# Twenty idle transposes per step on TensorE in the first stage of a recommender scoring kernel

## The chip, the cores and the metric

The kernel runs on one core of one Trainium2 chip. The metric is the device time of one execution in microseconds (us), as the median of several runs.

## What is computed

There are 1024 sequences of 50 item numbers, and a table of 100001 items by 128 numbers whose row 0 counts as zero. The reference, cut to what matters:

```python
emb = emb_table.at[0].set(0.0)
e = emb[seq]                                   # 1024 x 50 x 128
prefix = jnp.cumsum(e, axis=1)
uF = prefix / jnp.minimum(t_idx, lengths)      # running mean per step
mean, var = uF.mean(axis=0), uF.var(axis=0)    # over the 1024 sequences
y = (uF - mean) * lax.rsqrt(var + BN_EPS) * gamma + beta
def step(v, x):                                # 50 steps, one after the other
    v = v + (x - v) / TAU
    spike = (v - V_TH >= 0)
    return v - spike * V_TH, spike
_, spikes = lax.scan(step, v0, moveaxis(y, 1, 0))
scores = spikes.mean(axis=0) @ emb.T           # 1024 x 100001
```

## The kernel before

The program has two stages. The **first stage** walks through the 50 steps and counts spikes; the **second stage** multiplies the counts by the table and writes 410 MB of scores. The order of instructions on every engine is the order of the Python code: it is written out by hand, and no planner moves anything.

In the first stage the layout is 128 features on the partitions and 1024 sequences along the free dimension, in two halves of 512. A step `t` works like this:

- **Gather.** POOL issues eight indirect DMAs (line 207), each of which fetches 128 table rows into a piece of the tile `e_t`. The pool `gather` has two buffers. `gather(t + 2)` stands behind step `t`'s transposes in the code and takes the buffer of `e_t`, so its first DMA waits until TensorE (PE) has finished with `e_t`.
- **Transposes.** PE transposes the eight pieces onto a running sum in PSUM, `pre[0]` and `pre[1]` (line 324, four pieces for each half). Each transpose waits for its own piece to land.
- **Running mean.** VectorE (DVE) turns each half of `pre` into `uF` (line 335) and takes its statistics (line 336). The first `uF` of a step waits for the fourth transpose, the second for the eighth.
- **Corrections.** `correct(t + 1, l)` (line 282) issues two matmuls of 128x512 onto `pre`, which take the table's row 0 out again where a sequence has item 0. Each of them overwrites what `uF` has just read, so it waits for that `uF`.
- **Rest of the step.** DVE and ScalarE (ACT) make the scale, the membrane value `v`, the count and the part that is left over (lines 342 to 379, 294, 298 and 301). They need neither PE nor POOL.

So on PE one step is: eight transposes of `e_t`, two corrections for step `t + 1`, eight transposes of `e_{t+1}`, and so on. In steps 42 and 44 the function `prepare` (lines 136, 152, 153) puts another eight transposes, of table rows into a PSUM tile `pt`, behind the corrections; ACT and DVE copy that tile.

PSUM has eight banks: two for `pre`, four for the two `v` tiles, and two for a tile `warm`. `warm` is written by a helper that is used in the last step only, and nobody reads it:

```python
def keep_busy(tile, times):
    for k in range(times):
        nc.tensor.transpose(warm[:, k % KQ * P : (k % KQ + 1) * P], tile, ident)
```

`KQ` is 8 and `P` is 128. In the second stage PE multiplies parts of the table by the counts, ACT and DVE take turns in copying PSUM to SBUF, and SP's queue writes the scores.

Of the kernel before, what the change touches and what calls it, by code (L numbers as in the profile page):

```python
# [24 lines left out]
KQ = HALF // P  # L25
# [14 lines left out]
def rec_kernel(  # L40
# [34 lines left out]
    ident = const.tile([P, P], F32, tag="ident", name="ident")  # L75
# [96 lines left out]
    with ExitStack() as ph:  # L172
# [107 lines left out]
        def correct(t, l):  # L280
            for h in range(B // BANK):
                nc.tensor.matmul(  # L282
                    pre[h],
                    lhsT=l,
                    rhs=zT[:, h * BANK : (h + 1) * BANK],
                    start=t == 0,
                    stop=False,
                    skip_group_check=True,
                )
# [18 lines left out]
# [3 lines that stand above are left out]
# [6 lines left out]
        for t in range(T):  # L317
# [20 lines left out]
                gather(t + 2)  # L338
            if not last:
                correct(t + 1, l)  # L340
            mv = sp.tile([P, 2], F32, tag="mv", name=f"mv_{t}")
            nc.vector.bn_aggr(mv, bs.rearrange("p h s -> p (h s)"))  # L342

# [210 lines left out]
```

## Time and profile before

| what | value |
|---|---|
| median of 3 runs | 1633.66 us (1633.3 to 1634.7) |
| the profiled execution: device time | 1638.64 us |
| the profiled execution: span from first to last instruction | 1636.8 us |
| last gather of the first stage issued at | 564.2 us |
| mean granted TensorE clock over the span | 0.799 |
| busy share PE / DVE / ACT / POOL | 66% / 58% / 41% / 23% |
| written to HBM | 409.6 MB |

A profile shows one execution. Busy shares are averages over both stages, so they say little about either of them. In the page's row of 40 slices each slice is 40.9 us long: the first 14 slices are the first stage, in which POOL is busy, and in the others POOL has nothing to do and the DMA engines move about 420 GB/s. The times of a PE instruction in the profile are those of its start, and of an end that is modelled and not observed.

### The profile page before, as it was taken

To read this page: it belongs to the slowest core of one execution; us is meant where nothing else is said; L and a number is where in the kernel's file an instruction comes from. 1 tells how busy PE (TensorE), PEld (TensorE's weight loads), DVE (VectorE), ACT (ScalarE), POOL (GpSimd) and SP (SyncE) were. 2 spreads that over 40 slices of the span, in tenths; PEclk is the share of its full clock that TensorE was granted. 3 is DMA by queue.
4 is the path that set the end of the run, shared out by engine and by line. 5 is a ranking of instruction groups with operands and counts; after the bars stand their busy time and mean duration, and the time that the engine had idled before them with its cause. 6 is when DMAs were issued, how large, how long until landed. Compare 5 with 4: busy or idle time off the path is not lost.

```text
span 1636.8 us, 12254 instructions
## 1 busy us (share of the span) xinstructions
PE 1085.8 (66%) x4464; PEld 806.9 (49%) x4464; DVE 948.7 (58%) x1127; ACT 673.0 (41%) x697; POOL 381.1 (23%) x406
## 2 busy tenths in 40 slices
PE   4333332333332488888988877888878888788884
PEld 2212111222112366666766666666666666566663
DVE  5666654677665865665755554555545555555652
ACT  2333322333323354555554444444444444444442
POOL 7666666766666500000000000000000000000000
PEclk7555555555555599999999999989999999999998
DMA  9611111111111279999999999999999999999998
GB/s 346 240 46 46 46 45 46 51 45 47 45 46 47 66 326 412 415 423 412 405 426 430 427 428 429 403 432 426 418 428 420 408 423 426 427 424 408 429 401 358
DMA packets 51313, 488.12 MB, mean 298 GB/s; under 512 B 10079, under 2 KB 10336, under 8 KB 30004
## 3 DMA queue, kind: packets, MB, share of 16 engines
q1 hardware_dynamic: 30752, 430.86, 62.6%
q0 software_dynamic: 12800, 26.24, 5.4%
q10 hardware_dynamic: 7700, 30.23, 4.5%
q8 instruction: 35, 0.57, 0.1%
q14 instruction: 26, 0.21, 0.0%
HBM read 77.69 MB, written 409.60 MB: 298 GB/s over the span
## 4 chain that ended last, share of the span: by engine, by line
DMA 42%; PE 16%; DVE 14%; another core or an unknown queue 9%; POOL 7%; issue 5%; ACT 5%; ACTq 0%; SPq 0%; DVEq 0%; POOLq 0%
DMA scores<-o 40%; PE po L160 14%; POOL e L207 7%; DVE o L512 3%; ACT o L514 3%; DVE uF L335 2%; DVE bs L336 2%; DMA e<-in_L_rec_emb_table,idx 2%; DVE v L379 2%; DVE negv L298 1%; ACT v L376 1%; PE pre L324 1%; DVE count L301 1%; DVE pairs L153 1%
## 5 line engine op out<-in xcount | busy, mean ns | idle before, releaser
L512 DVE TENSOR_SCALAR o<-po 128x1024 f32<-128x1024 f32 (+1 forms) x391 | 467.4, 1214 | 326.0 <-DMA scores<-o 183.8
L514 ACT ACTIVATE o<-po 128x1024 f32<-128x1024 f32 x391 | 391.8, 1025 | 503.9 <-DMA scores<-o 358.6
L207 POOL DMA_INDIRECT e<-in_L_rec_emb_table,idx x400 | 380.4, 951 | 183.5 <-issue 110.9
L160 PE MATMUL po<-pairs,countB 128*128 128x512 f32 (+1 forms) x1120 | 291.2, 406 | 61.1 <-ACT o L514 61.1
L160 PE MATMUL po<-pairs,countC 128*128 128x512 f32 (+1 forms) x840 | 237.8, 430 | 59.0 <-ACT o L514 53.1
L160 PEld LDWEIGHTS po<-pairs,countB 128*128 128x128 f32 x1120 | 210.4, 193 | 122.0 <-ACT o L514 80.0
L282 PE MATMUL pre<-zT,ls 128*128 128x512 f32 x100 | 78.4, 786 | 271.2 <-DVE uF L335 227.2
L160 PEld LDWEIGHTS po<-pairs,countC 128*128 128x128 f32 x840 | 166.2, 205 | 111.0 <-ACT o L514 65.0
L282 PEld LDWEIGHTS pre<-zT,ls 128*128 128x128 f32 x100 | 29.0, 291 | 309.9 <-DVE uF L335 255.7
L324 PE MATMUL pre<-ident,e 128*128 128x128 f32 x400 | 126.8, 435 | 79.5 <-DMA e<-in_L_rec_emb_table,idx 63.0
L335 DVE SCALAR_TENSOR_TENSOR uF<-rlen,pre 128x512 f32<-128x512 f32 x100 | 68.0, 680 | 161.7 <-remote 124.4
L324 PEld LDWEIGHTS pre<-ident,e 128*128 128x128 f32 x400 | 80.4, 209 | 126.8 <-DMA e<-in_L_rec_emb_table,idx 94.7
L153 DVE TENSOR_TENSOR pairs<-pt,pairs 128x1024 fp32r<-128x1024 f32 x70 | 85.3, 1218 | 96.1 <-ACT pairs L152 96.0
L346 ACT ACTIVATE r<-mv,eps 128x1 f32<-128x1 f32 x50 | 14.8, 295 | 273.0 <-DVE mv L342 181.0
L136 PE MATMUL pt<-ident,rows 128*128 128x128 f32 (+1 forms) x768 | 105.6, 283 | 9.9 <-issue 4.9
L136 PEld LDWEIGHTS pt<-ident,rows 128*128 128x128 f32 (+1 forms) x768 | 95.1, 148 | 27.4 <-issue 11.5
L160 PE MATMUL po<-hi,countB 128*128 128x512 f32 x208 | 85.4, 411 | 13.9 <-ACT o L514 13.6
L152 ACT CAST pairs<-pt 128x1024 fp32r<-128x1024 f32 x70 | 70.1, 1013 | 41.0 <-PE pt L136 41.0
L160 PE MATMUL po<-lo,countB 128*128 128x512 f32 x208 | 83.2, 400 | 0.0
L294 ACT ACTIVATE d<-v,less 128x1024 bf16<-128x1024 f32 x49 | 54.5, 1113 | 65.4 <-DVE v L379 36.3
L160 PE MATMUL po<-hi,countC 128*128 128x512 f32 x156 | 66.5, 426 | 14.2 <-ACT o L514 12.6
L376 ACT ACTIVATE v<-uF,hgb,a 128x1024 f32<-128x1024 f32 x49 | 59.2, 1208 | 31.0 <-DVE a L372 11.7
(88 smaller groups left out, 887.2 us busy)
## 6 DMA issues: line engine op xcount, KB each, us to landing
scores<-o SPq DMA_DIRECT2D x96, 3072.0 KB
scores<-o SPq DMA_DIRECT2D x32, 1536.0 KB
scores<-o SPq DMA_DIRECT2D x30, 1024.0 KB
rows<-in_L_rec_emb_table ACTq DMA_DIRECT2D x19, 1536.0 KB
scores<-o SPq DMA_DIRECT2D x8, 2896.5 KB
rows<-in_L_rec_emb_table SPq DMA_DIRECT2D x5, 3072.0 KB
e<-in_L_rec_emb_table,idx POOLq DMA_INDIRECT x400
rows<-in_L_rec_emb_table SPq DMA_DIRECT2D x2, 1024.0 KB
```

The source lines that it names most:

```text
L136: nc.tensor.transpose(pt[:, k0 : k0 + pw], r[:pw, k0 : k0 + D], ident[:pw, :pw])
L152: nc.scalar.copy(vh, vp)
L153: nc.vector.tensor_tensor(vl, vp, vh.bitcast(F32), ALU.subtract)
L160: nc.tensor.matmul(po[:, :kw], lhsT=counts[n], rhs=part[:, k0 : k0 + kw], start=j == 0, stop=j == 1,)
L207: nc.gpsimd.indirect_dma_start(out=es[t][:, n * P : (n + 1) * P], out_offset=None, in_=table, in_offset=bass.IndirectOffsetOnAxis(ap=idx[: ...
L282: nc.tensor.matmul(pre[h], lhsT=l, rhs=zT[:, h * BANK : (h + 1) * BANK], start=t == 0, stop=False, skip_group_check=True,)
L294: nc.scalar.activation(d, v, AF.Identity, bias=less)
L324: nc.tensor.matmul(pre[h][:, k : k + P], lhsT=e[:, h * BANK + k : h * BANK + k + P], rhs=ident, start=False, stop=last, is_transpose=True, ...
L335: nc.vector.scalar_tensor_tensor(uF[:, cs], rlen[:, cs], 1.0 / (t + 1), pre[h], ALU.max, ALU.mult)
L376: nc.scalar.activation(vt, uF[:, cs], AF.Identity, bias=hgb[:, 1:2], scale=a)
L512: nc.vector.tensor_scalar_mul(o[:, h0 : h0 + hw], po[:, :hw], 1.0 / T)
L514: nc.scalar.mul(o[:, h0 : h0 + hw], po[:, :hw], 1.0 / T)
```

## The change

One line is added behind the corrections of each step but the last:

```diff
             if not last:
                 correct(t + 1, l)
+                keep_busy(ident, 2 * KQ + KQ // 2)
             mv = sp.tile([P, 2], F32, tag="mv", name=f"mv_{t}")
             nc.vector.bn_aggr(mv, bs.rearrange("p h s -> p (h s)"))
```

In 49 steps PE gets twenty more transposes of the identity (line 310), each a weight load and a 128x128 matmul in float32, written to the two banks of `warm`. They wait for nothing, nobody waits for them, and nobody reads what they write. On PE they stand between the corrections for step `t + 1` and the transposes of `e_{t+1}`. The instructions of the other engines are the same, in the same order. Behind that line, all line numbers of the changed kernel are higher by one.

## The prediction

> **What bounds the kernel now.** I read the page's slices first. POOL works in the first 14 slices of 40.9 us; from there on the DMA row stands at 9 with about 420 GB/s. The second stage is bound by writing 409.6 MB and the change does not touch it, so a microsecond that the first stage ends later is a microsecond on the total. Then the groups.
>
> ```profile
> POOL 7666666766666500000000000000000000000000
> PEclk7555555555555599999999999989999999999998
> ...
> L207 POOL DMA_INDIRECT e<-in_L_rec_emb_table,idx x400 | 380.4, 951 | 183.5 <-issue 110.9
> ...
> L335 DVE SCALAR_TENSOR_TENSOR uF<-rlen,pre 128x512 f32<-128x512 f32 x100 | 68.0, 680 | 161.7 <-remote 124.4
> ```
>
> A gather takes 0.95 us and the next starts 0.30 us later (110.9 us of "issue" over 364 gaps): 1.25 us each, 10.0 us for the eight of a step. 400 of them fill 499 us, but the last one is issued at 564.2. So POOL's stream sets the end of the stage, and about 60 us of it are gaps. The waits tell which:
>
> ```profile
> POOL e L207 <- remote: 50.0, 10, 5.8
> POOL e L207 <- PE pre L282: 13.7, 3, 5.4
> ...
> DVE uF L335 <- remote: 124.4, 18, 10.0
> ```
>
> Thirteen times POOL stands for 2.5 to 5.8 us, 63.7 us in all. It waits for PE to be done with the buffer of two steps before. DVE's `uF` waits for PE too, up to 10 us. Yet PE is mostly idle. The timeline of steps 42 and 43, where `prepare` has eight more transposes, shows the riddle:
>
> ```profile
> 490.67 0.80 PE L282 MATMUL pre<-zT,ls 128*128 128x512 f32 x1 [1.14 <-DVE uF L335]
> ...
> 496.34 1.94 PE L136 MATMUL pt<-ident,rows 128*128 128x128 f32 x8 [4.87 <-issue]
> ...
> 498.07 1.80 PE L324 MATMUL pre<-ident,e 128*128 128x128 f32 x8
> ...
> 506.12 0.95 POOL L207 DMA_INDIRECT e<-in_L_rec_emb_table,idx  x1 [0.30 <-issue]
> 512.33 1.01 ACT L152 CAST hi<-pt 128x1024 fp32r<-128x1024 f32 x1 [15.11 <-remote]
> 512.84 0.94 POOL L207 DMA_INDIRECT e<-in_L_rec_emb_table,idx  x1 [5.76 <-remote]
> 513.37 1.22 DVE L153 TENSOR_TENSOR lo<-pt,hi 128x1024 fp32r<-128x1024 f32 x1 [17.14 <-ACT hi L152]
> 514.51 0.68 DVE L335 SCALAR_TENSOR_TENSOR uF<-rlen,pre 128x512 f32<-128x512 f32 x1
> ```
>
> By its records PE is through with all sixteen transposes at 499.9. Everyone who waits for them starts at 512.3 or later: the copy of `pt`, POOL, `uF`. PE reports its work done 12 us late, and does so 5.2 us after POOL has issued its last gather (507.07). In all of the long stalls POOL stops first and PE's reports come some 4 to 6 us later. In the trace's semaphore updates of such stretches PE reports one instruction per 2.1 to 2.8 us (325.9 and 328.7, say) while gathers run, then a handful within 0.2 us once they have stopped.
>
> When does this come? I counted PE's instructions between the stalls. From one restart of POOL to the next stop there are mostly four sets of gathers, 39.6 to 39.9 us, and 39 or 40 PE instructions (ten per step). The lag shows from about the 28th on. After the restart at 512.84 the second `prepare` comes early, and POOL stops after two sets, 19.7 us, with 28 instructions:
>
> ```profile
> 517.15 1.91 PE L324 MATMUL pre<-ident,e 128*128 128x128 f32 x8
> ...
> 528.75 1.94 PE L136 MATMUL pt<-ident,rows 128*128 128x128 f32 x8 [3.31 <-DVE count L301]
> 530.48 1.91 PE L324 MATMUL pre<-ident,e 128*128 128x128 f32 x8
> ...
> 533.76 0.69 DVE L335 SCALAR_TENSOR_TENSOR uF<-rlen,pre 128x512 f32<-128x512 f32 x1 [0.42 <-PE pre L324]
> ```
>
> Here PE ran sixteen transposes in one go, and the fourth of the `e` ones (start 531.12) was reported at 533.74. I read this as a **backlog**: reports leave at one per 2.45 us while gathers run, and some 20 may be outstanding (28 in 19 us less 19/2.45 = 8; 32 in 24 us less 10) before PE's progress becomes visible only at that rate. The stop of the gathers empties it. What holds the reports up the trace does not name; that the count is of instructions, whether they signal or not, rests on the two `prepare` steps, since of the eight transposes of `pt` only the last signals.
>
> **What the Trainium skill says.** "Perfetto Trace Analysis", Per-instruction lifecycle, Tensor Engine Instruction: the profile's end of a matmul is computed, and the semaphore goes out only once PSUM has acknowledged the write. The trace agrees: 499.9 against 512.3. "TensorE: Matmul & The Clock Gate", Part 1: the array runs at half clock until it has been busy for about 3.4 us. The PEclk row agrees (5 through the stage). Part 4 of that page says that transposes don't count for this; the windows disagree, as the sixteen transposes are followed by one window at full clock, though reports still stood still in it:
>
> ```profile
> 496.20:499.60 3.40, 3.26 (x16) 3.27 (x16) 0.04 (x1) 1.01 (x1) 2.77 (x3) 0.50 0.20 58
> 499.60:503.00 3.40, 0.27 (x2) 0.00 (x0) 0.00 (x0) 0.00 (x0) 2.50 (x3) 1.00 0.19 55
> ```
>
> **The change part by part.** Nothing is removed or moved; 49 x 20 = 980 transposes are added. Back to back, one starts each 0.213 us at half clock (eight in 1.91 us with the last one's 0.42), so twenty hold PE for 4.3 us, or about half of that where the clock rises. Behind them on PE stand the transposes of `e_{t+1}` (and `pt` in steps 42 and 44), and behind these the next corrections; DVE's `uF` and POOL's `gather(t + 3)` wait for those transposes.
>
> *As PE time it costs nothing.* Where nothing is late, `uF` starts every 7.35 us (301.70, 309.05), bound by DVE. With twenty more between, from `uF` of half 0: 2.0 us to the second correction, 0.6 for it, 4.3, three transposes (0.64), 0.5 to the report: 8.0 us. The gathers take 10.0, so POOL covers it. If that cover is gone, the price is 0.65 us a step.
>
> *As backlog it costs.* A step goes from 10 to 30 PE instructions. After an emptying, two corrections, twenty idle ones and the first transposes of `e_{t+1}` reach the limit within some 7 us (22 less 3). The eighth transpose is then not reported while the eight gathers in progress run, and POOL stops behind every set rather than behind every fourth. One set lasts 10.0 + 5.0 us. The 5.0 is the usual stall (4.5 to 5.8, mean 5.3 of the eleven long ones) less the 0.3 of an ordinary gap. Sets 2 to 49 wait for a buffer; I leave out the first two of these, where the backlog only builds up: 46 x 5.0 = 230 us. Of before, 63.7 - 13 x 0.3 = 60 us go. Sum: **+170 us**. On the profiled execution that is a span of 1807 and a device time of 1809; the median of the runs is 5.0 below the profiled one, so 1804. The last step and the second stage stay as they are. Bounds of the unknown stall: 2.5 us (the shortest) gives 46 x 2.2 - 60 = +41; 7.5 us, if more unreported work takes longer to clear, gives 46 x 7.2 - 60 = +271.
>
> **The rivals.**
> 1. *Idle transposes cure the stalls.* The late reports often begin when PE is nearly idle, one transpose per landing gather; a PE that is kept busy would report at once. Then POOL never stops: -60 us, 1574. It needs only that the density of PE's work decides, in the wait of line 207. Against it: sixteen in a row at 528.75 were late at once, and sixteen at 496.34, full clock included, freed nothing. The point from which it decides: fewer than 13 stalls are left.
> 2. *Only instructions that signal or wait count.* Then PE's idle time hides all: within 3 us, about 1634. For it speaks that idle ones carry no semaphores; against it, the `pt` transposes, seven of eight without.
> 3. *A larger limit for plain instructions.* POOL stops behind every second set: 24 x 5.0 - 60 = +60, 1694.
> 4. *Longer stalls*, as bounded above: 1905, or more.
>
> **How the numbers follow.** Backlog with a stall per set 0.58, every second set 0.11, longer stalls 0.10, the cure 0.17, hidden 0.04. The likeliest gives 1804. The range reaches from just under the +41 bound to the +271 one, 1665 to 1905, which takes in the first two and part of the third; the cure stays out. 0.2% (3.3 us) is what a measurement of this kernel can tell from no change. Faster 0.17, same 0.04, slower 0.79.
>
> **What would show it.** Right: POOL's waits at line 207 rise from 63.7 us to some 240 in about 46 stalls of 5 us; the last gather is issued near 735; each step lasts about 15 us; the second stage has the same length; PEclk rises above 5 in the first stage without a gain. Wrong: few stalls of POOL and a last gather near 505 (rival 1), or the same 13 stalls (rival 2).

## The result, and the profile after

| | before | after |
|---|---|---|
| median of 4 runs (lowest to highest) | 1634.18 us (1633.3 to 1635.9) | 1652.13 us (1649.55 to 1653.23) |
| ratio over all runs, with its 95% interval | | 1.0099 (1.0087 to 1.0111) |
| profiled execution: device time, span | 1638.64, 1636.8 us | 1651.82, 1650.0 us |
| granted clock over the span | 0.799 | 0.867 |
| POOL standing over 1 us ahead of a gather | 13 times, 63.7 us | 24 times, 72.9 us |
| end of the last gather | 565.1 us | 572.9 us |
| end of the last `uF` | 572.9 us | 587.2 us |

The kernel became 1.0% slower. The forecast was 10.4% (1804 us), with a range that began at 1665. The direction was right and the size was not. (The ratio is not formed from the two medians, whose quotient is 1.011; the same holds for the ratios below.)

The page of the changed kernel, its slices and its groups (busy us, mean ns | idle before, releaser):

```profile
POOL 7666766667666500000000000000000000000000
PEclk8677767677768699999999999989999899999998
...
L207 POOL DMA_INDIRECT e<-in_L_rec_emb_table,idx x400 | 381.8, 954 | 189.8 <-issue 110.6
...
L335 DVE SCALAR_TENSOR_TENSOR uF<-rlen,pre 128x512 f32<-128x512 f32 x100 | 67.8, 678 | 184.4 <-remote 172.0
```

The gathers are as long as before, and POOL's idle time has grown by 6.3 us only (183.5 to 189.8). The idle time ahead of `uF` has grown by 22.7 us to 184.4, and nearly all of it is a wait for PE (172.0 us of it stand as "remote", a releaser that the trace does not name). The first stage's clock went from 5 to between 6 and 8, without a gain. The waits of the changed kernel (sum in us, times, longest):

```profile
DVE uF L335 <- remote: 172.0, 23, 9.6
...
POOL e L207 <- remote: 71.5, 23, 4.5
...
POOL e L207 <- PE pre L324: 1.4, 1, 1.4
```

So the number of stalls about doubled, but their mean fell from 4.9 to 3.0 us. The timeline of one pair of sets shows the new pattern:

```profile
97.69 3.47 PE L310 MATMUL warm<-ident 128*128 128x128 f32 x20
...
101.00 1.04 PE L324 MATMUL pre<-ident,e 128*128 128x128 f32 x8
...
102.40 0.68 DVE L335 SCALAR_TENSOR_TENSOR uF<-rlen,pre 128x512 f32<-128x512 f32 x1
...
103.72 0.67 DVE L335 SCALAR_TENSOR_TENSOR uF<-rlen,pre 128x512 f32<-128x512 f32 x1
...
104.79 2.35 PE L310 MATMUL warm<-ident 128*128 128x128 f32 x20
...
106.97 1.04 PE L324 MATMUL pre<-ident,e 128*128 128x128 f32 x8
...
114.17 0.95 POOL L207 DMA_INDIRECT e<-in_L_rec_emb_table,idx  x1 [0.31 <-issue]
117.98 0.69 DVE L335 SCALAR_TENSOR_TENSOR uF<-rlen,pre 128x512 f32<-128x512 f32 x1 [8.14 <-remote]
118.35 0.94 POOL L207 DMA_INDIRECT e<-in_L_rec_emb_table,idx  x1 [3.24 <-remote]
```

The first set of `e` transposes behind twenty idle ones is reported at once (101.00, the two `uF` at 102.40 and 103.72). The second set is through by its records at 108.01, but `uF`, which waits for the fourth of it, starts ten microseconds later, after POOL's last gather has ended at 115.12. From stall to stall there are two sets of gathers and 60 PE instructions, twenty times in a row.

In the profiled executions the span grew by 13.2 us, and it divides like this:

- The last gather ends 7.8 us later (565.1 to 572.9).
- From there to the end of the last `uF` it takes 14.3 us instead of 7.8: +6.5. The `uF` of half 0 in the last step but one is the first thing behind a late report; it starts at 575.98, when the gathers are over, and all the rest of the two steps comes after it. Before, the last late report came at 563.0 and for half 1, ahead of the last gather.
- The second stage takes 1062.8 us instead of 1063.9: -1.1.

The medians differ by 18.0 us, since the profiled execution of before lies 4.5 us above its own median and that of after at its own.

### The profile page after: what moved, and what is told of

Read it like the earlier page. It is cut to its first block, busy times and chain, and to the rows that moved or that the text cites. A ratio compares the mean times of both kernels' runs of the same rounds, so it can differ in the third digit from the quotient of the medians.

```text
span 1650.0 us, 14214 instructions
## 1 busy us (share of the span) xinstructions
PE 1167.8 (71%) x5444; PEld 934.6 (57%) x5444; DVE 948.3 (57%) x1127; ACT 673.8 (41%) x697; POOL 382.5 (23%) x406
## 4 chain that ended last, share of the span: by engine, by line
DMA 41%; DVE 20%; PE 17%; another core or an unknown queue 11%; ACT 6%; issue 3%; POOL 1%; ACTq 0%; SPq 0%; DVEq 0%
DMA scores<-o 40%; PE po L160 14%; DVE uF L335 4%; DVE bs L336 4%; DVE o L513 3%; DVE v L380 3%; ACT o L515 3%; DVE negv L298 2%; PE warm L310 2%; ACT v L377 2%; POOL e L207 1%; DVE pairs L153 1%; DVE count L301 1%; DVE a L373 1%
## 5 line engine op out<-in xcount | busy, mean ns | idle before, releaser
L207 POOL DMA_INDIRECT e<-in_L_rec_emb_table,idx x400 | 381.8, 954 | 189.8 <-issue 110.6
L282 PE MATMUL pre<-zT,ls 128*128 128x512 f32 x100 | 65.7, 659 | 288.9 <-DVE uF L335 274.5
L282 PEld LDWEIGHTS pre<-zT,ls 128*128 128x128 f32 x100 | 24.0, 241 | 321.2 <-DVE uF L335 303.1
L335 DVE SCALAR_TENSOR_TENSOR uF<-rlen,pre 128x512 f32<-128x512 f32 x100 | 67.8, 678 | 184.4 <-remote 172.0
L310 PE MATMUL warm<-ident 128*128 128x128 f32 x992 | 170.0, 348 | 0.0
L310 PEld LDWEIGHTS warm<-ident 128*128 128x128 f32 x992 | 164.0, 186 | 6.6 <-issue 5.1
```

Of the source, the lines that this page charges most:

```text
L207: nc.gpsimd.indirect_dma_start(out=es[t][:, n * P : (n + 1) * P], out_offset=None, in_=table, in_offset=bass.IndirectOffsetOnAxis(ap=idx[: ...
L282: nc.tensor.matmul(pre[h], lhsT=l, rhs=zT[:, h * BANK : (h + 1) * BANK], start=t == 0, stop=False, skip_group_check=True,)
L335: nc.vector.scalar_tensor_tensor(uF[:, cs], rlen[:, cs], 1.0 / (t + 1), pre[h], ALU.max, ALU.mult)
```

## The experiments

The stalls below are counted in the trace: every gap of over 1 us between two gathers of line 207 (a line some numbers higher where a kernel has more lines). "A set" is the eight gathers of one step. The edits are cut to the lines that matter; the tile `idle` in some of them is a new one that nobody reads. Each ratio is to the kernel before as it ran beside that experiment: its median was 1640.38 us beside the first four, 1636.48 beside the next four and 1636.06 beside the last four.

In the first four expectations A says that the **count** of PE's instructions decides when POOL stops, and B that what decides is the **time** for which the idle ones hold PE. All four replace the added line.

**Eight instead of twenty.**

```diff
-                keep_busy(ident, 2 * KQ + KQ // 2)
+                keep_busy(ident, KQ)
```

> Eight idle transposes per step in the place of twenty. Theory A (PE's late reports are a backlog counted in PE instructions, an idle one counting about a third, since it neither waits nor signals): POOL stops behind every third set of gathers (16 stalls of 3 to 5 us), within 10 us of the kernel before. Theory B (what counts is the time that PE is held between the corrections and the next transposes, 4.3 us with twenty): 1.7 us is too little to matter, POOL stops behind every fourth set as before, 13 stalls, the time of before within 3 us.

Measured: 1651.9 us, 1.0058 (1.0039 to 1.0076). There were 23 stalls, 71.1 us in all: some after three sets and 54 PE instructions (3.8 to 4.6 us), others in pairs: 1.5 to 1.7 us after two sets and then 3.0 to 3.3 us after one more, together somewhat more than a stall after three sets takes. Forty per cent of the idle instructions bring nearly the stalls of twenty, so the cost is not in proportion to the count. B falls. A had 16 stalls and at most 10 us; the loss was 11.5 us.

**Forty instead of twenty.**

```diff
-                keep_busy(ident, 2 * KQ + KQ // 2)
+                keep_busy(ident, 5 * KQ)
```

> Forty idle transposes per step. Theory A: the backlog is full in each step, POOL stops behind nearly every set of gathers: 46 stalls of 3 us against 24 with twenty, so 60 to 80 us slower than before. Theory B: PE is held for 4.5 to 8.5 us per step; the same stalls as with twenty, and some us more where the transposes come too late for VectorE: 20 to 40 us slower than before.

Measured: 1669.2 us, 1.0170 (1.0152 to 1.0189). Now POOL stops behind every set, 47 times, as the prediction had it for twenty. But a stall is 2.1 us, not 5 and not 3:

```profile
POOL e L207 <- remote: 79.0, 37, 3.7
POOL e L207 <- PE pre L324: 20.3, 10, 2.2
```

The 47 stalls sum to 99.3 us. A got the count and not the length. B's time fits and its picture of the stalls does not. This is where the constant length of a stall fell.

**Seven long matmuls instead of twenty short ones**: a similar time on PE (mostly 3.2 us in a row, where the twenty take 2.3 to 4.5), a third of the instructions.

```diff
-                keep_busy(ident, 2 * KQ + KQ // 2)
+                for k in range(KQ - 1):
+                    nc.tensor.matmul(warm[:, :BANK], lhsT=zT[:, :P], rhs=zT[:, :BANK], start=True, stop=True)
```

> Seven idle matmuls of 128x512 in the place of the twenty transposes: PE is held for about as long (7 x 0.6 = 4.2 us at half clock) by a third of the instructions. Theory A: as eight idle transposes, a stall behind every third set, within 10 us of before. Theory B: as twenty transposes, a stall of 3 us behind every second set, 15 to 20 us slower than before.

Measured: 1651.13 us, 1.0064 (1.0046 to 1.0081). POOL stops every third set, after 51 PE instructions, twelve times in a row, for 4.5 us; 16 stalls, 69.8 us. That is A's count; the loss of 10.8 us is just over the 10 that A allowed. B had a stall behind every second set.

```profile
206.51 3.19 PE L342 MATMUL warm<-zT 128*128 128x512 f32 x7
```

**Twenty transposes of 16x16.**

```diff
-                keep_busy(ident, 2 * KQ + KQ // 2)
+                for k in range(2 * KQ + KQ // 2):
+                    nc.tensor.transpose(warm[:16, k % KQ * P : k % KQ * P + 16], ident[:16, :16], ident[:16, :16])
```

> Twenty idle transposes of 16x16 in the place of 128x128: as many instructions, in a quarter of the time or less. Theory A: a stall behind every second set as with twenty large ones, 15 to 20 us slower than before. Theory B: as before the change, 13 stalls, the time of before within 3 us.

Measured: 1657.56 us, 1.0102 (1.0084 to 1.0120), with 24 stalls of 3.3 us on average, 79.5 us, every second set and every 60 instructions as in the changed kernel. The loss of 17.2 us is the one that A had. Its timeline, its waits and its slices:

```profile
202.82 0.70 PE L342 MATMUL warm<-ident 16*16 16x16 f32 x20
203.45 1.97 PE L324 MATMUL pre<-ident,e 128*128 128x128 f32 x8
```

```profile
POOL e L207 <- remote: 79.5, 24, 3.6
```

```profile
PEclk7555555555555589999999999999998999999998
```

The twenty hold PE for 0.7 us and not 2.3 to 4.5, the clock stays at 5, and the stalls come just as often. B is out: neither PE's time nor the clock decides how often they come. The count does.

**What the four lengths say.** I put the length of a stall against the sets of gathers since the last one:

| sets since the last stall | kernel | stall |
|---|---|---|
| 1 | forty | 2.1 us (45 stalls) |
| 2 | twenty | 3.1 us (20) |
| 3 | seven long | 4.5 us (12) |
| 4 | before | 5.3 to 5.8 us (8) |

These are the common cases; a stall that came out short (2.5 us after four sets in the kernel before) was followed by a long one (4.5 us after one more). The length does not follow the count of PE's instructions, which is 50, 60, 51 and 40 from stall to stall in the order of the table. A line through 146 stalls (all but the first two of each of these kernels, of those with the eight and with the small transposes and of the one with ScalarE's copies below; r = 0.88) is 1.1 us and another 1.03 us for each set. For 49 sets that makes 50.5 us however they are divided, and 1.1 us for each stall: 65, 68, 77 and 102 us for 13, 16, 24 and 47 stalls, against 63.7, 69.8, 72.9 (79.5 with the small ones) and 99.3 measured. I took this as theory **D, the debt**: while gathers follow each other in 1.25 us, something falls behind by some 0.13 us per gather. PE's reports come through when it has caught up, for which the gathers have to stop. The count of PE instructions decides only how often that is asked. If D holds, then time given to POOL's gathers ahead of the waits takes the stalls away, and the idle transposes are then free. By the bare count they stay as often as they were.

**A pause behind each set, without and with the twenty.** POOL fills an unused tile six times ahead of each step's gathers from step 2 on, once on the kernel before and once on the changed one:

```diff
+            if t > 1:
+                for _ in range(6):
+                    nc.gpsimd.memset(idle, 0.0)
```

> The kernel before, with a pause of POOL of 1.2 to 1.5 us (six memsets of 128x128 on a tile that nobody reads) ahead of each step's gathers. In the runs so far the length of a stall is 1.0 us plus 0.11 us per us of gathers since the last one, so the stalls sum up to about 55 us plus 1 us for each of them. Theory D (the gathers run up a debt of 1.1 us a set that has to be worked off before PE's reports get through; how often POOL is stopped for it follows the count of PE instructions): the pauses pay the debt, the 13 stalls vanish or get shorter than 2 us, and the time stays within 10 us of before. Theory A (the backlog is PE's alone and empties only when the gathers have stopped for 3 to 5 us): the stalls stay as they are and the pauses come on top, 60 to 75 us slower.

> The changed kernel with the same pause of POOL ahead of each step's gathers. Theory D: with the debt paid in each step PE's reports are prompt however many there are; the twenty idle transposes cost nothing any more, and the time is that of the kernel before with the pause, within 5 us. Theory A: 24 stalls of 3 us on top of the pauses, 70 us slower than before.

Measured: 1663.18 us, 1.0153 (1.0127 to 1.0179) without the twenty, and 1661.19 us, 1.0140 (1.0114 to 1.0166) with them. The timeline of the first, and the waits of the second:

```profile
202.91 1.53 POOL L209 MEMSET idle<- 128x128 f32 x6
204.96 0.95 POOL L211 DMA_INDIRECT e<-in_L_rec_emb_table,idx  x1 [0.52 <-PE pre L328]
```

```profile
POOL e L211 <- PE pre L328: 16.6, 32, 0.5
```

Both have a gap of 2.05 us ahead of each of 48 sets, and no wait of POOL for PE is longer than 0.5 us. The twenty transposes, which cost 18 us in the kernel as it is, cost nothing here: the kernel with them is even 2 us faster. A, which wanted a stop of 3 to 5 us, is out. But forty's stalls are no longer than these pauses (2.1 us), so the two runs do not tell D from a backlog that any stop of some 2 us empties. As a time D missed: the pauses and one more gap of 2.1 us inside a set cost 86 us beyond ordinary gaps and save 60, so the last gather ends at 593.0 us instead of 565.1, and the kernel is 26.7 us slower where I had put it within 10.

**A slower pitch**: POOL fills 64 columns ahead of each gather, on the kernel before.

```diff
+                if t > 1:
+                    nc.gpsimd.memset(idle[:, :64], 0.0)
```

> The kernel before, with one short memset of 128x64 ahead of each single gather, so that a gather takes some 0.15 to 0.2 us longer. Theory D: at a pitch of 1.39 us or more no debt comes up; no stalls at all, and the last gather is issued at 400 times the pitch plus some 15 us. Theory A: the stalls stay, as there are ten PE instructions per step as before, and the longer pitch comes on top.

Measured: 1637.58 us, 1.0012 (1.0001 to 1.0024). The pitch went to 1.283 us only. There were 27 gaps left, mean 1.9 us, 51.1 us in all; the last gather ended at 565.5. So 0.033 us more for each of 400 gathers, 13 us, took as much from the stalls. D's condition, a pitch of 1.39, was not reached.

**Half of the gathers**, on the changed kernel; pieces 4 to 7 are not fetched from the third step on, and the transposes of half 1 then read the pieces of half 0 (a second edit, not shown), so the scores are no longer those of the reference.

```diff
-            for n in range(NB):
+            for n in range(NB // 2 if t > 1 else NB):
```

> The changed kernel with half of the gathers left out from the third step on (pieces 4 to 7 are not fetched, the transposes of the second half read pieces 0 to 3 once more): the steps are then bound by VectorE's chain of 7.35 us or, with the idle transposes, 8.0 us. Theory D: POOL is idle for 2.4 us or more of each step, four times the debt of a half set; PE reports promptly, no stall, and the first stage takes about 400 us in the place of 560. Theory A: 30 PE instructions in 8 us fill the backlog, VectorE's waits for PE of 5 to 10 us remain in every second step.

Measured: 1467.98 us, 0.8958 (0.8934 to 0.8982). The last `uF` ends at 404.0 us. With the same PE instructions, twenty idle ones in each step, late reports all but vanish:

```profile
POOL e L207 <- PE pre L324: 133.2, 45, 5.9
...
DVE uF L335 <- PE pre L324: 9.4, 8, 4.6
```

The longest wait of `uF`, 4.6 us, is in the second step, ahead of which the gathers are still whole. POOL stands often here because the steps are now set by VectorE and buffers come free at its pace. PE's count alone makes no late reports; it takes the gathers.

**Short pauses** of three fills (a gap of 1.3 us), without and with the twenty:

```diff
+            if t > 1:
+                for _ in range(3):
+                    nc.gpsimd.memset(idle, 0.0)
```

> The kernel before with three memsets of 128x128 on POOL ahead of each step's gathers in the place of six: a pause of 1.0 us more than an ordinary gap, close to the debt of 1.1 us a set. Theory D: most of the 13 stalls vanish and what is left is short; 50 x (10.0 + 1.0) + 15 = 565 at the most for the last gather, so 3 to 12 us faster than before, since the 1 us that each stall costs besides the debt goes. Theory A: 13 stalls as before and 48 us of pauses on top.

> The changed kernel with the same pause of three memsets. Theory D: within 5 us of the one without idle transposes as far as the debt is paid; where 0.1 us a set stays open, some stalls of 1.5 to 2 us come back, up to 10 us more. Theory A: 24 stalls of 3 us and the pauses on top, 60 us slower than before.

Measured: 1642.64 us, 1.0042 (1.0025 to 1.0058), and 1648.0 us, 1.0073 (1.0051 to 1.0094). Five stalls of 3.0 to 4.0 us were left in the first, twelve of 2.6 to 3.1 us in the second. Beyond the ordinary 0.3 us, pauses and stalls together take 60 and 68 us, much as the stalls of before and of the changed kernel do alone (60 and 66). So the pauses took the place of most stalls and did not save time: the last gathers ended at 565.9 and 575.2 us. (The trace of the first is of an execution of 1636.13 us, 6.5 below the median.) D missed here in both: it had the first kernel 3 to 12 us faster, and the stalls that are left short (1.5 to 2 us in the second), since nearly the whole debt is paid in each set. The line of 1.03 us per set holds for kernels without pauses only.

**A pitch of 1.365 us**, by fills of 160 columns ahead of each gather, on the kernel before:

```diff
+                if t > 1:
+                    nc.gpsimd.memset(idle, 0.0)
```

> The kernel before with a memset of 128x160 ahead of each single gather, for a pitch of some 1.4 us. Theory D: that is over the 1.39 us at which no debt comes up; no stall of POOL, and the last gather at 400 x pitch + 15 us, so 565 to 590. Theory A: the stalls stay and come on top.

Measured: 1636.63 us, 0.9998 (0.9981 to 1.0015). Twelve gaps of 1.1 to 2.9 us were left, 20.3 us in all, and the last gather ended at 567.4. D had none from 1.39 on, which this run just misses, so it is no test of that figure.

**Twelve small copies on ScalarE** in each step, on the kernel before, to see whether any engine's instructions count:

```diff
+                for k in range(12):
+                    nc.scalar.copy(idle[:, k : k + 1], less)
```

> The kernel before with twelve idle copies of 128x1 on ScalarE at the end of each step, and nothing added on PE. If the count of every engine's instructions decides how often POOL is stopped, the stalls come behind every second or third set, 16 to 24 of them, and some 5 to 15 us are lost. If it is PE's count alone, there are 13 stalls as before and the time stays within 3 us, unless the copies delay ScalarE's own work, which the step of 10 us covers.

Measured: 1642.17 us, 1.0038 (1.0027 to 1.0050). Its waits and its slices:

```profile
POOL e L208 <- remote: 37.2, 9, 5.5
POOL e L208 <- PE pre L283: 25.8, 5, 5.4
```

```profile
PEclk9999999999996599999999999999998999999998
```

There are 13 stalls, 62.2 us, and the last gather ends at 564.8: the stalls of before, so ScalarE's instructions do not count. The 9 of the clock row is not to be believed here: the trace has no record of the clock before 501.8 us, and eight `e` transposes in a row still take 1.91 us as at half clock, where the changed kernel at full clock takes 1.04. The time missed the 3 us that were expected. The loss is behind the gathers, where the last `uF` ends 11.2 us after the last gather instead of 7.8.

**What the last gather says.** With stalls left alone, the last gather ended at 565.1 us (before) and 564.8 (ScalarE); with a pitch of 1.283 at 565.5; with short pauses at 565.9; with a pitch of 1.365 at 567.4. None ended earlier. Whether the time is given as stalls, as pauses or as a slower pitch, the 400 gathers, the first of which starts at 3.4 to 3.6 us, take 62 to 65 us more than 499 us, which is 400 times the pitch of 1.25 us. Asking for reports more often adds to that (the changed kernel 572.9, forty 590.8), and paying too much does too (593.0). No version that fetches all rows is faster than the kernel before.

**What does not fall behind.** An obvious candidate for the debt would be the gathered rows, landing later and later. The DMA packets in the traces say no: in the set ahead of a stall, the last packet of a gather ends 1.18 us (before) and 1.24 us (the changed kernel) after POOL's instruction, as the median, and in the set behind a stall 1.19 and 1.24 us.

## Why the prediction was wrong in size

- **What bounds the kernel: right.** POOL's stream of gathers sets the end of the first stage, and reports that PE gives late are what stops it. The second stage did not change (-1.1 us).
- **As PE time the twenty cost nothing: right.** With PE's time cut from 2.3 to 4.5 us per step to 0.7 the loss was the same, and with long pauses between the sets the twenty were free.
- **The count decides how often: right in kind.** Idle ones that signal nothing count too, so rival 2 falls; rival 1, the cure, falls with 24 stalls instead of 13; rival 4, longer stalls, with 3.0 us.
- **The limit, "some 20 may be outstanding": failed.** With twenty idle transposes in each step every second set is stopped, not every set: 24 stalls and not 46. After an emptying, 30 instructions within 8 us (95.8 to 103.7: two corrections, twenty idle ones, the eight transposes at 101.00) were still reported at once, where the prediction let 22 less 3 fill the backlog. Rival 3, at 0.11, had this count, and its +60 was still far too much. A stall behind each set took forty.
- **The length of a stall, "the 5.0 is the usual stall": failed, and is the larger error.** It was taken as constant, since the trace of before had eleven long stalls that agreed, but eight of them came after four sets of gathers. It also held one after two sets, 3.0 us, and a pair of 2.5 and 4.5 us; I took the shortest as a bound and did not set the lengths against the sets. Without pauses a stall is 1.1 us and 1.03 us per set. With 24 stalls instead of 46 the prediction's 5.0 would still have given +60. With the 2.1 us of a stall after one set, 46 of them would have given 46 x (2.1 - 0.3) - 60 = +23, and in the forty kernel, which has such stalls, the last gather did end 25.7 us later.
- **The lower end of the range** rested on 46 stalls of 2.2 us each (+41), both terms at once; with 24 of the short ones it would have been 24 x 2.2 - 60 = -7. The price of a stall and their number are tied to each other, and I varied them as if they were not.
- **"The last step and the second stage stay as they are": failed for the last step**, by 6.5 us. A late report in the last step but one now comes only after the gathers have ended, and VectorE's chain of two steps stands behind it. It is half of the growth of the span. That the direction came out right owes something to this and so to luck: with the stalls that came, the prediction's own sum is only 24 x (3.0 - 0.3) - 60 = +5.
- **PEclk above 5 without a gain: right**, and shown apart by the small transposes (5, stalls just as often).

What the Trainium skill says in "Perfetto Trace Analysis", Per-instruction lifecycle, Tensor Engine Instruction, that the end of a matmul in a profile is computed, held: 108.01 by the record, 117.98 for the engine that waits. That the gap can be ten microseconds these runs show.

What stays open is what the debt is in. The trace names no resource: the reports stop, and gathers and transposes go on. That it needs the gathers is shown (with half of them, or with long enough pauses between them, the long stalls are gone), as is that the number of PE's instructions sets how often POOL is stopped. That gathers run up a debt, at a fixed rate that a pause pays back, is a picture: it fits the sums and not the lengths of the stalls left by short pauses, and since a set always takes 10 us it cannot be told from one that runs up with time. Gathers of fewer rows, and plain DMAs in their place, would tell whether it grows with rows or with instructions; neither was tried. Nor is the limit known. POOL waits only between sets, so 40, 54, 51, 60 and 50 instructions from stall to stall (before, eight, seven long, twenty, forty) are whole multiples of a step's 10, 18, 17, 30 and 50. A limit of some 37 to 40, an idle instruction counted as any other, would give these spacings, and with eight idle ones two sets make 36, which may be why that kernel mixes two and three. This is an estimate from the counts, and it leaves out the stop after 28 behind the second `prepare` and four stops after 30 in the ScalarE kernel.

## What to carry to other kernels

Work that costs an engine nothing can still use up something its reports need, so count the instructions you add to an engine that others wait for, and not only their time. Before you multiply a new number of stalls by the length of the old ones, plot the old lengths against what ran since the last stall: if they grow with it, as here, stalls that come twice as often are also shorter, and only the fixed part of each is added. Look also at which late report is the last one before a stage ends, because there no work is left to cover it.

## What the runs showed of the hardware that was not expected

- **Indirect gathers at 1.25 us apiece hold TensorE's reports back.** Most late reports came some 10 us after the modelled end in the changed kernel (11.8 at the end of the stage) and up to 13.7 us in the one before. From the third step on, those of the changed kernel all came while POOL stood or after its last gather; in the one before some also came while gathers ran.
- **Their sustained pitch was longer than the one they are issued at.** In the traces 400 gathers ended no earlier than 564.8 us, be it with stalls, pauses or a slower pitch: from the first one's start at 3.5 us that is 1.40 us each. What sets it the traces do not say.
- **Transposes of 128x128 raise the granted clock.** The Trainium skill, in "TensorE: Matmul & The Clock Gate", Part 4, says that they do not count for it. The measurement decides: the changed kernel's first stage went from 5 to between 6 and 8 and its mean clock from 0.799 to 0.867, and behind twenty idle ones the transposes of `e` mostly start every 0.109 us, against 0.213 at half clock. Transposes of 16x16 did not do it (0.795).
- **A 9 in the row of the clock can be no measurement.** Three traces without added PE work (both slower pitches and ScalarE's copies) show 9 in nearly all slices of the first stage and a mean clock of 0.941 to 0.956. Their first records of the clock stand at 566.5, 532.5 and 501.8 us, and ahead of these, transposes in a row still start every 0.213 us. The spacing of the instructions tells the speed.
